# A four-stage convolution kernel: layer 1 with TensorE in a fixed order, the squares of x2 on ScalarE, weight and x2 loads issued apart

## The chip, the cores and the metric

The kernel runs on one core of a Trainium2 chip. The metric is the device time of one execution in microseconds (us). The parts of a time are read from the profiled execution of the same kernel, so they add up to its span and not exactly to the median.

## The reference

The input is 16 images of 256 channels, 28 x 28 pixels. Four layers follow each other. Layer 0 is a binary 3x3 convolution with a batch norm over all images. Layer 2 is two binary 3x3 convolutions with batch norms, layer 3 is attention over the pixels. Layer 1, for each image:

```python
residual = prelu(x, a_alpha1)
z = hardsign(x + a_move)
y = prelu(bn(conv3x3(z, clip(a_w)), a_bn1), a_alpha2)
mix = s * x + y * (1 - s)
y = se_gate(mix) * y                # mean over pixels -> 256 to 32 -> relu -> 256 -> sigmoid
y = bn(y * residual, a_bn2) + residual          # called x2 until the last line below
z2 = hardsign(y + f_move)
u = prelu(bn(conv1x1(z2, clip(f_w)), f_bn1), f_alpha2)
mix2 = s2 * y + (1 - s2) * u
return bn(se_gate(mix2) * u, f_bn2) + y         # x2, the input of layer 2
```

Layer 2 begins with a batch norm of x2 over all 16 images, so it needs the sums of x2 and of its squares.

## The kernel before

Layer 1's 3x3 convolution is done in a form with four transformed rows `vs` (u = 0 to 3). An image has two halves `mo` of the output channels, a half has two pairs, (1,2) and (0,3), and a pair is 24 matmuls of 0.19 us: 96 matmuls, 18.4 us per image. A pair fills one PSUM buffer, each half of the 1x1 (8 matmuls) one more, and there are three such buffers. VectorE and ScalarE turn pairs into rows, PReLU, sums for the gate, the gates themselves, x2, and the next image's input. The loop is software-pipelined: image b's 3x3, image b-1's gate, x2 and 1x1, image b-2's second gate. `hid` and `gate` are the names of the gate's two small matmul groups.

```python
for b in range(B + 2):
    # now: b < B;  one: 0 <= b-1 < B;  two: 0 <= b-2 < B;  ahead: b+1 < B
    conv_pair(b, 0, ...)        # pair (1,2) of half 0
    unit_a(b - 2)               # 1x1's result: u, and its relu rn, on ScalarE
    enter(b + 1)
    unit_b(b - 2)               # PReLU of u, with its sum for the gate
    sum_pair(b, 0); conv_pair(b, 0, 0, 0)
    h = gates_hidden(b)         # sums -> hid (TensorE) -> relu (ScalarE)
    conv_pair(b, 0, 1, 3)
    transform(b + 1)            # next image's vs
    g = gates(h)                # gate (TensorE) -> four sigmoids -> scaling
    branch1_a(b - 1, g); rows_out(b, 0); branch1_b(b - 1); load_x(b + 2)
    ...                         # half 1: pair (1,2), prelu_out(b, 0), residual, sum_pair
    conv_pair(b, 1, ...)        # pair (0,3) of half 1
    branch2(b - 2, g)           # x2 complete, bn_stats of it on VectorE, stored
    conv1x1(b - 1)
    rows_out(b, 1); prelu_out(b, 1)
    ...                         # one step of layer 2's weights in images 2 to 6
```

(The conditions `if now` and so on are cut.) A scheduler decides at build time in which order each engine gets its instructions; the statements only give it a priority. So TensorE's order need not be the order of the text.

## Time and profile before

| part, from the profiled execution | us |
|---|---|
| layer 1's loop: first 3x3 matmul (164.66) to the end of the last (528.17) | 363.5 |
| drain: from there to layer 2's first matmul (563.52) | 35.3 |
| entry: layer 2's first binary convolution, up to the start of the second (724.61) | 161.1 |
| everything else (layer 0 ahead, second binary convolution and attention behind) | 618 |
| median of the runs | 1179.3 |

The first three rows are what the change touches. Two more lines than the prediction shows are needed. The first is the page's summary of the chain that ended last, its share of the span by engine:

```profile
PE 64%; DVE 14%; ACT 3%; DMA 2%; issue 1%; SPq 0%; DVEq 0%; ACTq 0%
```

The second is the windows view over one late image (from, to, length, then busy us and instructions of TensorE, weight loads, VectorE, ScalarE, GpSimd, then clock, DMA share and GB/s):

```profile
401.71:425.10 23.39, 22.40 (x121) 21.71 (x120) 21.80 (x42) 14.78 (x22) 0.53 (x1) 1.00 0.25 87
```

VectorE is busy 21.8 of 23.4 us: it hardly has air, which fits the 14% of the chain that are its own.

### The profile page before, as it was taken

How to read it: one execution, taken by the hardware profiler on the slowest of the kernel's cores; microseconds unless marked ns; L12 is line 12 of the kernel's file. 1: busy time of each engine (PE TensorE's matmuls, PEld its weight loads, DVE VectorE, ACT ScalarE, POOL GpSimd, SP SyncE). 2: the span in 40 equal slices, each digit the busy share in tenths (PEclk: the TensorE clock that was granted, in tenths of full speed). 3: DMA queues.
4: the chain of work that ended last, by engine and by line, in shares of the span. 5: the costliest groups of instructions: out<-in, count | busy, mean ns of one | idle time of the engine just before them, and what ended most of it. 6: DMA issues, size and time to landing. Idle time of an engine off the chain costs nothing.

```text
span 1178.2 us, 15695 instructions
## 1 busy us (share of the span) xinstructions
PE 1113.0 (94%) x6015; PEld 944.0 (80%) x6019; DVE 817.7 (69%) x1438; ACT 692.3 (59%) x1041; POOL 142.7 (12%) x139
## 2 busy tenths in 40 slices
PE   6999999999999999994889999999999999999995
PEld 6999989999899989993789998999965545545542
DVE  3854378999999999875366665666683676576665
ACT  5644536667766665654455553555567767767752
POOL 2000000000100000000000000000004434434421
PEclk9999999999999999996989999999999999999998
DMA  7643331223221321011930000000013453553522
GB/s 283 217 163 125 136 111 55 69 83 127 92 83 69 107 87 68 28 48 37 410 115 32 1 1 1 1 1 1 1 41 97 110 164 110 137 163 119 131 82 84
DMA packets 25968, 111.62 MB, mean 95 GB/s; under 512 B 3552, under 2 KB 6304, under 8 KB 25888
## 3 DMA queue, kind: packets, MB, share of 16 engines
q1 hardware_dynamic: 20432, 80.85, 19.6%
q0 software_dynamic: 5456, 29.71, 8.7%
q8 instruction: 49, 0.80, 0.3%
q14 instruction: 31, 0.25, 0.1%
HBM read 65.59 MB, written 44.96 MB: 94 GB/s over the span
## 4 chain that ended last, share of the span: by engine, by line
PE 64%; DVE 14%; ACT 3%; DMA 2%; issue 1%; SPq 0%; DVEq 0%; ACTq 0%
PE cv L239 20%; PE cv L543 16%; PE sc L946 7%; PE av L967 6%; PE mi L931 4%; PE sm L1007 4%; DVE x L672 2%; DVE x L627 2%; DVE l_parts L674 2%; DVE xs L535 2%; PE cv L258 2%; PE mi L1017 2%; DVE y L576 1%; DMA st<-in_w2b_dram 1%; DMA p<-x2d 1%
## 5 line engine op out<-in xcount | busy, mean ns | idle before, releaser
L543 PE MATMUL cv<-vs,w 128*128 128x392 f32 x1536 | 302.3, 355 | 11.4 <-DVE y L576 10.6
L239 PE MATMUL cv<-fpads,wpk 128*128 128x392 f32 x1440 | 295.3, 358 | 12.5 <-DVE wpk L190 10.0
L543 PEld LDWEIGHTS cv<-vs,w 128*128 128x128 f32 x1536 | 286.1, 190 | 17.4 <-DVE y L576 14.9
L239 PEld LDWEIGHTS cv<-fpads,wpk 128*128 128x128 f32 x1440 | 273.2, 193 | 17.3 <-issue 10.4
L788 DVE SCALAR_TENSOR_TENSOR p<-r,r,cv 128x392 f32<-128x392 f32 x128 | 78.6, 614 | 80.4 <-ACT r L785 80.4
L950 ACT ACTIVATE es<-sc 112x784 f32<-112x784 f32 x112 | 87.4, 822 | 74.1 <-PE sc L946 73.9
L239 PE MATMUL cv<-fpads,wpl 128*128 128x392 f32 x576 | 124.8, 352 | 0.0
L239 PEld LDWEIGHTS cv<-fpads,wpl 128*128 128x128 f32 x576 | 108.8, 190 | 0.6
L250 ACT ACTIVATE t<-cv,rounding 128x392 f32<-128x392 f32 x96 | 56.2, 586 | 86.5 <-PE cv L239 81.7
L251 DVE TENSOR_SCALAR up<-t 128x392 fp32r<-128x392 f32 x96 | 35.0, 364 | 84.4 <-ACT t L250 84.4
L946 PE MATMUL sc<-q,k 64*112 64x392 f32 x448 | 90.5, 518 | 2.2 <-DVE k L938 1.6
L785 ACT ACTIVATE r<-cv 128x784 f32<-128x784 f32 (+1 forms) x66 | 52.9, 805 | 60.0 <-PE cv L258 58.1
L967 PE MATMUL av<-es,va 112*64 112x392 f32 x448 | 80.8, 499 | 0.0
L946 PEld LDWEIGHTS sc<-q,k 64*112 64x112 f32 x448 | 36.3, 174 | 43.5 <-issue 18.3
L960 POOL TENSOR_TENSOR sum<-sum,es 112x784 f32<-112x784 f32 x32 | 68.4, 2138 | 2.5
L967 PEld LDWEIGHTS av<-es,va 112*64 112x64 f32 x448 | 29.6, 136 | 47.4 <-issue 44.6
L103 DVE TENSOR_TENSOR vs<-pad 128x840 fp32r<-128x840 bf16 (+1 forms) x68 | 64.0, 975 | 0.9 <-ACT pad L514 0.9
L938 DVE COPY k<-mi 64x784 f32<-64x784 f32 x16 | 15.6, 976 | 66.3 <-ACT q L937 66.3
L449 ACT CAST n<-cv 128x784 int16<-128x784 f32 x32 | 26.0, 813 | 54.7 <-DVE l_parts L448 24.1
L640 PE MATMUL cv<-z,fw 128*128 128x392 f32 x256 | 51.4, 350 | 5.0 <-ACT z L631 5.0
L657 ACT ACTIVATE u<-cv,c_bn,s_bn 128x784 f32<-128x784 f32 x31 | 31.2, 1006 | 41.5 <-PE cv L640 41.5
L640 PEld LDWEIGHTS cv<-z,fw 128*128 128x128 f32 x256 | 46.9, 193 | 5.6 <-ACT z L631 5.5
(229 smaller groups left out, 1650.7 us busy)
## 6 DMA issues: line engine op xcount, KB each, us to landing
xs<-in_x_dram SPq DMA_DIRECT2D x32, 784.0 KB, 4.4
x2d<-x POOLq DMA_DIRECT2D x16, 784.0 KB, 3.6
xd<-p SPq DMA_DIRECT2D x16, 784.0 KB, 3.3
out_dram<-p SPq DMA_DIRECT2D x15, 784.0 KB, 5.2
p<-x2d SPq DMA_DIRECT2D x13, 784.0 KB, 15.6
p<-x2d POOLq DMA_DIRECT2D x13, 784.0 KB, 9.2
n0d<-n POOLq DMA_DIRECT2D x16, 392.0 KB, 2.7
n<-n0d SPq DMA_DIRECT2D x16, 392.0 KB, 3.1
```

The costliest lines, as they stand in the source:

```text
L103: V.tensor_tensor(o, a, b, op)
L239: T.matmul(pss[j][:, mo, :HN].rearrange("p (a b) -> p a b", b=S), lhsT=lhsT, rhs=pads[:, j // 2 % 2, k, r:r + HR, c:c + S], start=start, s ...
L250: A.activation(r, pss[j][:, 0, :HN], AF.Identity, bias=rounding, scale=1.0 / PACK)
L543: T.matmul(ps.rearrange("p (a b) -> p a b", b=S), lhsT=w[:, k, c, u, mo * P:(mo + 1) * P], rhs=vs[:, b % 2, u, k, :, c:c + S], start=(n == 0),
L640: T.matmul(ps[:, h, :HN], lhsT=w[:, k, mo * P:(mo + 1) * P], rhs=z2[b][:, k, h * HN:(h + 1) * HN], start=(n == 0), stop=(n == 3),)
L785: A.activation(r[:, mo], ps[:, mo, :HN], AF.Relu, scale=-1.0)
L788: V.scalar_tensor_tensor(p, r[:, mo], beta[:, mo:mo + 1], ps[:, mo, :HN], ALU.mult, ALU.add)
L931: T.matmul(ps[:, h, :HN], lhsT=wqk[:, k, :], rhs=x[b][:, k, h * HN:(h + 1) * HN], start=(k == 0), stop=(k == 1),)
L946: T.matmul(ps[:MC, h, :HN], lhsT=k_[rows, c * MC:(c + 1) * MC], rhs=qs[b][rows], start=True, stop=True)
L950: A.activation(e, ps[:MC, :, :HN], AF.Exp, scale=0.125)
L960: (V if late else nc.gpsimd).tensor_tensor(sums[b, late], sums[b, late], e, ALU.add)
L967: T.matmul(ps[64 * h:64 * h + 64, :HN], lhsT=w, rhs=e[:, h, :], start=start, stop=stop)
```

## The change

It has four parts, and each has its aim. (1) bn_stats of x2 leave VectorE; the sum of x2 rides on the operation that makes it, and the squares go to ScalarE. (2) In layer 1 TensorE gets exactly the order of the statements, and these are put into a new order: the gate right after the first pair, the 1x1 in the middle of the second half, the unit in the same iteration; fillers keep TensorE's clock up in the drain. (3) Loads of weights and of x2 are issued apart from the work, a few steps ahead. (4) The gate's biases become weight rows, so that one sigmoid serves four gates. Smaller edits go along: the 1x1 takes its matmuls by halves of `z`, in the last image one scaling of `y` moves to VectorE, and the two rows `up` and `vp` share one buffer, `uv`. The core of the diff:

```diff
@@ branch2: squares
-    V.scalar_tensor_tensor(v, us.pop((b, k))[0], g[:, k:k + 1], v, ALU.mult, ALU.add)
-    for i in range(2):
-        V.bn_stats(mom1.part(2 * b + i, k), v[:, i * HN:(i + 1) * HN])
+    V.scalar_tensor_tensor(v, us.pop((b, k))[0], g[:, k:k + 1], v, ALU.mult, ALU.add,
+                           accum_out=sum_x2[:, k, b:b + 1])
...
+    A.activation(full("rn", "square", 4), x2[b][:, k, :], AF.Square, bias=shift[:, k:k + 1],
+                 accum_out=sum_sq[:, k, b:b + 1])
@@ gates
-    for i, b2 in enumerate((pv("a_se_b2"), pv("f_se_b2"))):
-        for k in range(2):
-            A.activation(g[:, i, k:k + 1], ps[:, k, i:i + 1], AF.Sigmoid, bias=b2[:, k:k + 1])
+    A.activation(g.rearrange("p i k -> p k i"), ps, AF.Sigmoid)
@@ the loop (conditions cut)
-for b in range(B + 2):
+with tc.manual_schedule(engines={ET.PE}):
+  for b in range(B + 2):
     conv_pair(b, 0, ...)                     # pair (1,2); in the drain: keep_busy(14)
-    unit_a(b - 2); enter(b + 1); unit_b(b - 2)
-    sum_pair(b, 0); conv_pair(b, 0, 0, 0)
     h = gates_hidden(b)                      # now after 24 matmuls of the image
+    sum_pair(b, 0); conv_pair(b, 0, 0, 0)
+    enter(b + 1)
+    g = gates(h)                             # now after 36
     conv_pair(b, 0, 1, 3)
...
+    conv_pair(b, 1, ...)                     # pair (1,2) of half 1
+    prelu_out(b, 0); load_x(b + 2); transform(b + 1)
+    conv1x1(b - 1)                           # now after 72
+    late()                                   # sums of layer 2's weights
+    sum_pair(b, 1); conv_pair(b, 1, ...)     # pair (0,3)
+    unit_a(b - 1); residual(b + 1); rows_out(b, 1); unit_b(b - 1); prelu_out(b, 1)
@@ entry of layer 2
-for b in order[3:]:
-    x2[b] = pt[b]
-    nc.sync.dma_start(out=x2[b], in_=x2d[b])
+def sign2a(i, rows, out):
+    sign2(x2[order[i]], sg1, bg1, rows, out)
+    if rows.stop == S and i + 5 < B:
+        load_p(i + 5)
+for i in (3, 4):
+    load_p(i)
+...            # the first two weight loads of w2b are issued right behind these
```

## The prediction

> **What bounds the kernel now.** I read the page first (whose engine is full), then the stages, then the chain that ended last, then the timeline where it leaves TensorE.
>
> ```profile
> PE 1113.0 (94%) x6015; PEld 944.0 (80%) x6019; DVE 817.7 (69%) x1438; ACT 692.3 (59%) x1041; POOL 142.7 (12%) x139
> PEclk9999999999999999996989999999999999999998
> ```
>
> ```profile
> 594.50:857.00 262.50, 262.18 (x1382) 256.12 (x1383) 162.65 (x320) 138.39 (x181) 0.00 (x0) 0.99 0.05 14
> ```
>
> TensorE looks full, but the average hides layer 1 (about 160 to 562 us). The second fence is the windows view (start and end, length, then busy us of TensorE, weight loads, VectorE, ScalarE, GpSimd; clock; DMA): in the two binary convolutions TensorE really is full, 262.2 of 262.5 us. The clock row dips just once, at 530 to 560 us. So I split the time in three: layer 1's loop, its drain, the entry of layer 2.
>
> *Loop.* The chain of waits over one late image (start, us, what):
>
> ```profile
> 345.88 9.19 PE cv L543 x47
> 355.07 0.34 PE hid L477 x4
> ...
> 357.41 0.17 DVE gates L103
> ...
> 363.53 1.89 DVE xs L535 x2
> ...
> 366.89 1.48 DVE l_parts L674 x3
> 368.38 1.07 DVE y L576 x2
> 369.45 0.04 issue
> 369.49 2.54 PE cv L543 x12
> ```
>
> The image lasts 369.49 - 345.88 = 23.6 us. The last 12 us of it are VectorE working in order from the gates to the `y` that frees a PSUM buffer; the moments of x2 (bn_stats, L674) stand in front of that `y`. TensorE alone would need 18.4 us for 96 convolution matmuls (9.19 per 48), 2.86 for the 16 of the 1x1 and 0.7 for the gates: 21.9. The first image, which has neither, ends at 164.7 + 18.4 = 183.1; the fifteen from there to 528.2 took 345 us, 23.0 each. VectorE has little air, one wait of 1.55 us per image, for the sigmoid (timeline of another late image):
>
> ```profile
> 404.21 0.16 DVE L103 TENSOR_TENSOR gates<-gates,s_bn 128x4 f32<-128x4 f32 x1 [1.55 <-ACT gates L610]
> ```
>
> *Drain.* From the last 3x3 matmul (518.85 + 9.32 = 528.2) to layer 2's first (563.5) 35.3 us pass, mostly latency, and TensorE cools down:
>
> ```profile
> 505.68 3.03 PE L640 MATMUL cv<-z,fw 128*128 128x392 f32 x16
> 515.76 0.50 PE L477 MATMUL hid<-g,se 128*128 128x2 f32 x4
> ...
> 536.07 1.01 PE L477 MATMUL hid<-g,se 128*128 128x2 f32 x4 [5.04 <-DVE g L103]
> 543.66 4.78 PE L640 MATMUL cv<-z,fw 128*128 128x392 f32 x16 [4.96 <-ACT z L631]
> ```
>
> The same work takes 4.78 instead of 3.03 and 1.01 instead of 0.50.
>
> *Entry of layer 2.* The chain names two transfers, the TensorE timeline shows the hole:
>
> ```profile
> 562.00 14.33 DMA p<-x2d
> ...
> 576.41 14.66 DMA st<-in_w2b_dram
> ```
>
> ```profile
> 584.14 0.52 PE L258 MATMUL cv<-up,unpack 128*128 128x392 f32 x2
> 593.52 1.01 PE L207 MATMUL sumabs<-ones,ab 128*128 128x1 f32 x4 [8.87 <-DVE ab L201]
> 594.40 4.68 PE L239 MATMUL cv<-fpads,wpk 128*128 128x392 f32 x15
> ```
>
> The second convolution's weights were issued behind 13 loads of x2 (10 MB) and landed at 591. The first convolution runs from 563.52 to 717.4 = 153.8 us, the second, with no weights to make, from 724.61 to 863.1 = 138.5. So 15.4 us are lost: 8.9 idle, some 2 cold, the rest sums of weights between the steps.
>
> **What the Trainium skill says.** "DMA: Bandwidth & Descriptors", section "Queues, rings and completion order": on each DMA engine descriptors are consumed in ring order. The trace agrees: a 384 KB load that elsewhere lands in 3.7 us took 14.7 behind the x2 loads. "TensorE: Matmul & The Clock Gate", Part 1 (the HAM clock gate): idle for about 3.4 us the array falls to half clock; the trace's 0.50 to 1.01 agrees. The same page, "Architectural detail": ScalarE and VectorE are strict FIFO, which is why a bn_stats in front of `y` counts. "ScalarE: Activation LUTs", "What ACT_TABLE_LOAD costs": 280 ns + 0.833 N with a pointer bias, so 933 ns at N = 784 (the trace has 938 for such a Relu), and 1283 ns for a table load (trace 1.28 us).
>
> **The change, part by part.**
>
> 1. *Squares on ScalarE.* Four bn_stats per image leave VectorE, 4 x 0.47 = 1.9 us from start to start. Two Squares with an accumulator come to ScalarE. What an accumulator costs there, the attention shows:
>
> ```profile
> 954.50 0.50 ACT L1001 ACTIVATE junk<-sm 128x392 f32<-128x392 f32 x1
> 954.87 0.21 ACT L1001 ACTIVATION_READ_ACCUMULATOR junk<-sm 128x1 f32 x1
> 955.12 0.53 ACT L1001 ACTIVATE junk<-r 128x392 f32<-128x392 f32 x1
> ```
>
> The read follows 0.37 after the start and takes 0.25 to the next start. A Square of 784 should step like the Relus of that size, 0.84 to 0.89, and 0.25: two are 2.2 us per image. On VectorE the sum of x2 rides free: its operations with an accumulator step 0.95 as those without.
>
> 2. *Fixed order.* The gate's first matmuls move from behind 48 matmuls to behind 24, the 1x1 into the middle. The order of instructions shows what VectorE does then: rows out 1.07, two transforms 1.9, PReLU 0.95, sums 0.15, that is 4.07 us, before the gate's input is ready. I follow it from H, the start of the gate's first matmul, with the start-to-start steps of the trace. First matmul and 12 convolution matmuls 2.6, then second matmul, sigmoid (one for four) and scaling 1.1: VectorE goes on at H + 3.7. It then has 14.6 us (x2 1.9, x 1.92, rows 1.07, two transforms, PReLU and both halves of the next-but-one input 4.8, sums 1.1, two of unit 1.9, residual 1.9). Meanwhile ScalarE, which gets the rows at H + 8.7, has rn 0.8, squares 2.2, t 0.6, u and rn 1.8 in this order: unit's input is there at H + 14.1, where VectorE has been ready since 13.5; 0.6 wait. So the next image's rows start at 3.7 + 14.6 + 0.6 = H + 18.9 and the next gate at + 4.1 = 23.0. TensorE's own way: the sums of the pair end at H + 13.5 and free PSUM (0.8 after the 1x1 is done), plus 48 matmuls 9.2 = 22.7. I expect 23.0 us per image: the loop moves from PSUM to the gate, and little is gained against 23.4 to 24. In the five images that make layer 2's weights (sign and Abs ahead of rn on ScalarE, 1.6 us; packing 0.55 on VectorE) I get 24.1, where before the first of them ran at 22.7. Sum: first image 18.4, second 22.5, 5 x 24.1, 7 x 23.0, last two 22 each = 366 against 363.5 now (164.7 to 528.2), so about 3 us lost, 5 either way.
>
> 3. *Drain.* Counted from the last 3x3 matmul: rows and rn 2.1, PReLU and gate input 3.6, gates at 5.8 (one sigmoid for four, 0.26 for 0.72; warm), y 6.9, x 8.3, z 9.5, 1x1 from 9.6 to 12.6 (the first half of z suffices, warm), unit 15.8, gates 18.4, x2 20.4, squares 21.8. The table load for the root now stands behind the squares: 23.0; root and constants 1.5: 24.5; sign and first matmul 0.9: 25.4. Against 35.3 that is 10 us gained.
>
> 4. *Entry of layer 2.* Weights now stand behind five x2 loads and 0.4 MB, 4.4 MB. At the about 420 GB/s of this stretch they land 12 us after the issue, some 10 us after TensorE starts, and are wanted in the fifth step (about 16 us). No wait; of the 15.4 us stay the sums of weights, 7 x 0.45 = 3. Gain 12.
>
> 5. *Layer 0, bias rows, attention.* The early weight loads meet a TensorE that is already full (266 of 270 us busy between 30 and 300); 0. Bias rows are in point 3.
>
> Sum: 1179.9 + 3 - 10 - 12 = 1161.
>
> **Rivals.** (a) *TensorE becomes the bound in layer 1*: 21.9 per image if the wait in the loop is less than I add up. For it: VectorE's sum falls to 19.9, ScalarE's is 17; both under 21.9. Against it: VectorE stands idle between gate and sigmoid, as it does now (1.55 us per image), and more in the new order. It would end layer 1 some 14 us earlier: 1144 to 1148. (b) *ScalarE's squares are worse than 2.2 us, or collide with the weight steps*: 24 us per image, 10 us more, 1171. For it: rn and u stand behind them in order. (c) *The weight loads still come late*, because the queue waits for a buffer of x2 ahead of them: only 2 or 3 of the 12 us, 1170. Against it: those buffers are read in the first three images, before the weights are wanted. (d) *Cooling goes on*: the fillers end 1.5 us before the 1x1; a gap too short for it.
>
> **Range and chances.** The gains of drain and entry (22 us, give or take 3) I hold for safe; the loop is the open term, 5 us either way, and (a) is likelier than (b), since a fixed order was presumably chosen by looking. The 2% line is 1156.3, 5 us under my sum: 28% faster. Slower by 2% would need 1203: 1%. Eight in ten: 1150 to 1169.
>
> **What would show it.** In the loop: pitch of the images 23.0, and 24 in images 2 to 6; TensorE's waits named after the gate input `g` instead of `y`. A pitch near 22 says (a). In the drain: 25 us from the last 3x3 to layer 2, 1x1 at 3.0 us, no dip of the clock, the table load behind the squares. At the entry: no hole of 8.9 us, first convolution about 142 us. It would be wrong if layer 1's end moved by more than 8 us, or if a new wait for x2 loads came up in the first ten steps of layer 2.

## More of the kernel before

Every time quoted is a median of executions.

The loop ends with the last 3x3 matmul. Where the 1x1 stands behind an image's last pair, as in this kernel, the 1x1 of image 14 (about 3 us) therefore falls into the drain; where it stands in the middle of an image, it is counted in the loop.

## The result, and the profile after

The changed kernel took 1185.57 us (median of 4 runs, 1183.89 to 1187.65) against 1179.3 for the kernel before. The ratio is 1.0054, 95% interval 1.0035 to 1.0074: the same within 2%, but on the slow side, where 1161 had been predicted. Ratios here are the mean time of one kernel's fast runs over that of the other's fast runs of the same rounds, so not quite the ratio of the medians.

| part | before | predicted | after | change |
|---|---|---|---|---|
| loop | 363.5 | 366 | 390.6 | +27.1 |
| drain | 35.3 | 25.4 | 26.0 | -9.3 |
| entry | 161.1 | 149 | 151.5 | -9.6 |

The three changes sum to +8.2; the spans of the two profiled executions differ by 7.7. The changed kernel's profiled execution is the slowest of its four (1187.65 us), so a difference of 2 us between the parts of two kernels can lie in the execution. Drain and entry did about what they were meant to do. The loop is where the time went.

*Drain after*, TensorE's timeline (start, us, what, idle before it):

```profile
555.87 2.97 PE L346 MATMUL unused<-idle 128*128 128x512 bf16 x13
559.42 0.61 PE L507 MATMUL hid<-g,se 128*128 128x2 f32 x4 [0.58 <-DVE g L103]
...
565.62 3.23 PE L670 MATMUL cv<-z,fw 128*128 128x392 f32 x16
...
581.84 5.96 PE L252 MATMUL cv<-fpads,wpk 128*128 128x392 f32 x30
```

The fillers (`unused`) stand where TensorE had been idle, and the 1x1 takes 3.23 us where it took 4.78.

*Entry*, the windows view from the start of the first binary convolution to that of the second, first of the kernel before, then of the changed one:

```profile
563.52:724.61 161.09, 151.91 (x793) 145.62 (x794) 97.59 (x198) 80.10 (x107) 0.00 (x0) 0.97 0.25 94
```

```profile
581.84:733.30 151.46, 149.83 (x794) 143.65 (x794) 97.69 (x198) 80.71 (x108) 0.00 (x0) 1.00 0.26 101
```

TensorE's idle time in it falls from 9.2 to 1.6 us (length less busy time), and its own work is 2.1 us shorter because the clock stays at 1.00.

*Loop after.* The page's chain still gives VectorE a large share, and TensorE's timeline now shows it waiting in two places, ahead of the gate (16.7 us over the loop) and ahead of the last pair (6.8 us for `rn`):

```profile
PE 62%; DVE 16%; ACT 4%; issue 2%; DMA 2%; DVEq 0%; ACTq 0%
```

```profile
215.85 0.61 PE L507 MATMUL hid<-g,se 128*128 128x2 f32 x4 [1.50 <-DVE g L103]
216.32 3.49 PE L573 MATMUL cv<-vs,w 128*128 128x392 f32 x12
...
294.35 0.61 PE L507 MATMUL hid<-g,se 128*128 128x2 f32 x4 [1.82 <-DVE g L103]
...
418.28 0.61 PE L507 MATMUL hid<-g,se 128*128 128x2 f32 x4 [0.16 <-DVE g L103]
418.75 2.52 PE L573 MATMUL cv<-vs,w 128*128 128x392 f32 x12
...
432.20 9.37 PE L573 MATMUL cv<-vs,w 128*128 128x392 f32 x48 [0.79 <-ACT rn L533]
...
442.13 0.61 PE L507 MATMUL hid<-g,se 128*128 128x2 f32 x4 [0.56 <-DVE g L103]
```

From one `hid` to the next is one image: 442.13 - 418.28 = 23.85 us. In images 1 to 7, in most of which layer 2's weights are made too, it is 25.1 to 26.9. After six of the eight waits of 1.3 us or more the next 12 matmuls run slow, 3.49 instead of 2.52 in the lines above; the trace shows half the clock (0.50) granted for 3.4 us there.

The same image on VectorE (and the two squares on ScalarE):

```profile
421.85 0.16 DVE L103 TENSOR_TENSOR gates<-gates,s_bn 128x4 f32<-128x4 f32 x1 [1.82 <-ACT gates L638]
...
425.99 0.33 SPq L356 DMA_DIRECT2D xs<-in_x_dram  x1
...
427.83 0.94 ACT L707 ACTIVATE square<-x,shift 128x784 f32<-128x784 f32 x1
...
428.77 0.94 ACT L707 ACTIVATE square<-x,shift 128x784 f32<-128x784 f32 x1
...
429.70 0.66 ACT L594 ACTIVATE t<-cv,c_bn,s_bn 128x392 f32<-128x392 f32 x1
430.26 0.99 ACT L686 ACTIVATE u<-cv,c_bn,s_bn 128x784 f32<-128x784 f32 x1
430.90 1.03 DVE L541 SCALAR_TENSOR_TENSOR xs<-n,l_r,xs 128x784 f32<-128x784 int16 x1 [0.94 <-DMA xs<-in_x_dram]
431.15 0.99 ACT L533 ACTIVATE rn<-cv,nc,ns 128x784 f32<-128x784 f32 x1
```

Here VectorE waits 1.82 us for the gates, which the instruction next in its order needs, then 0.94 us for a load. Over the loop the waits for the gates come to 43.0 us, where it was 16.3 before, and those for the load to 7.3. The last pair's PSUM buffer is the 1x1's first half, which `rn` frees at 431.15 + 0.99 = 432.14; the pair starts at 432.20. The two squares stand ahead of `t`, `u` and `rn` on ScalarE. The windows view of the same image:

```profile
418.28:442.13 23.85, 22.49 (x120) 21.74 (x121) 20.34 (x38) 16.73 (x24) 0.53 (x1) 1.00 0.25 85
```

VectorE's work did fall, from 21.80 to 20.34 us per image. But the image did not get shorter. VectorE now stands idle 23.85 - 20.34 = 3.5 us in it, where it had been 1.6.

This gave four theories. T1: the fixed order puts the gate and the 1x1 in places where TensorE waits for VectorE's chain. T2: the squares on ScalarE hold up `t`, `u` and `rn`. T3: the sums for the weights come too late in the fixed order, and VectorE waits for them in line. T5: TensorE's slow clock after its waits is itself a large part. (T4, the wait for the load of `xs`, has no run of its own; it comes below.)

### The profile page after: what moved, and what is told of

Same layout as the page of the kernel before. It is cut to its first block, busy times and chain, and to the rows that moved or that the text cites. A ratio compares the mean times of both kernels' runs of the same rounds, so it can differ in the third digit from the quotient of the medians.

```text
span 1185.9 us, 15794 instructions
## 1 busy us (share of the span) xinstructions
PE 1129.0 (95%) x6069; PEld 954.7 (81%) x6075; DVE 794.7 (67%) x1410; ACT 714.2 (60%) x1053; POOL 146.0 (12%) x144
## 4 chain that ended last, share of the span: by engine, by line
PE 62%; DVE 16%; ACT 4%; issue 2%; DMA 2%; DVEq 0%; ACTq 0%
PE cv L252 20%; PE cv L573 12%; PE sc L1014 7%; PE av L1035 6%; PE mi L999 4%; PE sm L1075 4%; DVE vs L103 2%; PE unused L346 2%; PE cv L271 2%; PE mi L1085 2%; PE cv L670 2%; DMA xs<-in_x_dram 2%; DVE y L606 2%; DVE uv L596 2%; DVE xs L565 1%
## 5 line engine op out<-in xcount | busy, mean ns | idle before, releaser
L573 PE MATMUL cv<-vs,w 128*128 128x392 f32 x1536 | 309.9, 361 | 8.3 <-ACT rn L533 6.8
L573 PEld LDWEIGHTS cv<-vs,w 128*128 128x128 f32 x1536 | 293.0, 194 | 13.5 <-ACT rn L533 9.5
L264 DVE TENSOR_SCALAR uv<-t 128x392 fp32r<-128x392 f32 x96 | 35.0, 364 | 82.8 <-ACT t L263 82.8
L1075 PEld LDWEIGHTS sm<-wv,p 128*112 128x112 f32 x448 | 46.7, 178 | 5.0 <-issue 2.6
L1089 DVE TENSOR_TENSOR p<-mi,p 128x784 f32<-128x784 f32 x30 | 29.2, 974 | 31.5 <-PE mi L1085 31.1
L271 PE MATMUL cv<-uv,unpack 128*128 128x392 f32 x192 | 49.9, 341 | 0.0
```

The lines of the kernel that those rows point to most:

```text
L271: T.matmul(pss[j][:, mo, :HN], lhsT=unpack[mo], rhs=bs[j], start=False, stop=True, skip_group_check=(mo == 0))
L573: T.matmul(ps.rearrange("p (a b) -> p a b", b=S), lhsT=w[:, k, c, u, mo * P:(mo + 1) * P], rhs=vs[:, b % 2, u, k, :, c:c + S], start=(n == 0),
L1075: T.matmul(ps[:MC, c * 64:(c + 1) * 64], lhsT=x[b][:, k, c * MC:(c + 1) * MC], rhs=wv[:, k, :], start=(k == 0), stop=(k == 1),)
```

## The experiments

All sixteen kernels of the experiments gave correct results. Parts in us as in the tables above; the median of the runs last.

| run | loop | drain | entry | time |
|---|---|---|---|---|
| before | 363.5 | 35.3 | 161.1 | 1179.3 |
| changed | 390.6 | 26.0 | 151.5 | 1185.6 |
| entry only | 363.5 | 35.7 | 151.5 | 1168.6 |
| squares only | 350.0 | 38.1 | 160.0 | 1166.1 |
| changed, without squares | 393.0 | 26.0 | 151.7 | 1188.0 |
| changed, old loop | 348.3 | 32.1 | 151.5 | 1150.1 |
| gate 12 matmuls later | 386.3 | 27.4 | 151.5 | 1183.5 |
| weight sums first | 386.5 | 25.8 | 151.5 | 1182.6 |
| old statements, fixed order | 351.6 | 32.2 | 151.4 | 1154.9 |
| new statements, free order | 371.1 | 26.9 | 151.5 | 1168.9 |
| gate 24 later, 1x1 last | 350.7 | 31.3 | 151.5 | 1152.2 |
| squares late | 379.6 | 27.4 | 151.5 | 1176.7 |
| old loop, new last image | 351.6 | 27.4 | 151.5 | 1148.5 |
| the same, no fillers | 351.7 | 28.8 | 151.5 | 1150.9 |
| 1x1 last, gate early | 411.8 | 31.6 | 151.5 | 1216.1 |
| gate 12 later, squares late | 377.6 | 27.1 | 151.6 | 1175.6 |
| fillers ahead of the gate | 387.1 | 27.4 | 151.5 | 1186.0 |
| gate 24 later, 1x1 in the middle | 448.4 | 30.6 | 151.6 | 1243.4 |

### Which part of the change costs, and which pays

**Entry only.** The kernel before, with the loads issued apart in all layers and the entry's new order; loop, squares and gates untouched, but for the shared buffer `uv`.

```diff
 # the kernel before, plus:
+class Step: ...            # load() and work() apart
+steps = load_ahead(steps, 2)
+def sign2a(i, rows, out): ...   # the next x2 load behind each image's sign
```

> The kernel before with only the entry's part (loads apart from the work, x2 in steps, no drain or loop part). If the entry is worth the 9.4 us that the two traces show, the time is 1168 to 1172 us, the first binary convolution takes 143 to 146 us, and layer 1's loop stays at 363 to 365 us and the drain at 35. If the gain needs the new loop (x2 written earlier), the first binary convolution stays over 148 us and the time over 1174 us.

1168.56 us (ratio 0.9906, interval 0.989 to 0.9923), loop and drain as before, entry 151.5. The first binary convolution by itself, from its first matmul to its last, takes 144.9 us, where it took 154.5: as written. The entry's 9.6 us are there on their own, and they need nothing of the new loop.

**Squares only.**

```diff
 # the kernel before, plus:
-    V.bn_stats(mom1.part(2 * b + i, k), v[:, i * HN:(i + 1) * HN])
+    A.activation(..., x2[b][:, k, :], AF.Square, ..., accum_out=sum_sq[:, k, b:b + 1])
```

> The kernel before with only the squares moved from bn_stats on VectorE to ScalarE. Theory 1 (the fixed order is the cause of the longer loop): the loop gets 0 to 6 us shorter than 363.5, the time is 1173 to 1180 us. Theory 2 (squares on ScalarE are the cause, they hold up t, u and rn): the loop gets 5 us or more longer, 1184 us or more.

1166.13 us (ratio 0.9891, interval 0.9874 to 0.9907). The loop fell by 13.5 us, more than either theory had. T2 as a general statement has fallen: on ScalarE the squares do no harm in the old loop.

**Changed, without squares**: bn_stats back on VectorE, the new loop kept.

```diff
 # the changed kernel, with:
-    A.activation(..., x2[b][:, k, :], AF.Square, ..., accum_out=sum_sq[:, k, b:b + 1])
+    V.bn_stats(mom1.part(2 * b + i, k), v[:, i * HN:(i + 1) * HN])
```

> The changed kernel with bn_stats back on VectorE, the fixed order kept. Theory 1: the loop closes through VectorE and the gate, so with 1.9 us more on VectorE per image it gets longer still, 392 to 420 us, and the time is 1188 to 1215 us. Theory 2: the loop shrinks to 380 us or less, the time to 1175 us or less.

1187.96 us, loop 393.0. The time is just under what T1 had written, far from T2's. But VectorE's 1.9 us more per image, some 28 over the loop, show as 2.4 only: taking the squares off ScalarE also takes away what their place costs there (11 us, see *squares late*) and VectorE's waits for `xs`. **Changed, old loop** undoes the other factor: the old order of statements, TensorE free, everything else of the change kept.

```diff
 # the changed kernel, with:
-with tc.manual_schedule(engines={ET.PE}):
-    ...   # the new order
+for b in range(B + 2):
+    ...   # the order of the kernel before
```

> The changed kernel with the loop's old order of statements and TensorE's order left to the scheduler; squares on ScalarE, bias rows and the entry stay. Theory 1: the loop is 358 to 366 us again, the drain 32 to 36 us, the entry 9 us shorter than before: 1164 to 1171 us. Theory 2: the loop stays over 375 us and the time over 1178 us.

1150.14 us (ratio 0.9751, interval 0.9734 to 0.9767): 2.5% faster than the kernel before, and the loop even shorter than T1 expected. With the run *entry only* this makes a square of four loops:

| loop, us | bn_stats on VectorE | squares on ScalarE | gain of the squares |
|---|---|---|---|
| old loop | 363.5 | 348.3 | 15.2 |
| new loop | 393.0 | 390.6 | 2.4 |

So the new loop costs 42.3 us with the squares on ScalarE and 29.5 without, less the 6 and 10 us that it gives in the drain (about 3 us of each are only the 1x1 that is counted in the loop now): 36 and 20 us in all. The upper row is not the squares alone, because its two kernels also differ in the sigmoids and the small edits; the squares by themselves gave 13.5 us. And the new loop swallows the squares' gain. Why the old loop gets all of it shows the windows view of one image of that run, and its chain:

```profile
414.39:436.32 21.93, 21.93 (x121) 21.84 (x121) 20.18 (x39) 16.23 (x24) 0.53 (x1) 1.00 0.27 92
```

```profile
PE 74%; DVE 4%; ACT 3%; issue 2%; DMA 2%; POOL 1%; ACTq 0%; POOLq 0%; DVEq 0%
```

TensorE is busy 21.93 of 21.93 us. VectorE does the same 20.2 us of work as in the changed kernel, but TensorE bounds the loop, and VectorE's share of the chain is 4% instead of 16%.

### Is it fixing the order, or the order that was fixed?

**Gate 12 matmuls later.** The gate's groups after 36 and 48 matmuls of the image instead of 24 and 36.

```diff
+    sum_pair(b, 0); conv_pair(b, 0, 0, 0)
     h = gates_hidden(b)
-    sum_pair(b, 0); conv_pair(b, 0, 0, 0)
     enter(b + 1)
+    conv_pair(b, 0, 1, 3)
     g = gates(h)
-    conv_pair(b, 0, 1, 3)
```

> The changed kernel with the gate's two matmul groups 12 matmuls (about 2.4 us) later in the fixed order: the first after 36 matmuls of the image instead of 24, the second after 48 instead of 36. Theory 1 (TensorE stands still for the gate's sums, 17.3 us in 15 waits, and runs slow after it): those waits fall under 5 us, the 12 matmuls after them take 2.4 to 2.6 us again, the loop falls from 390.6 to 365 to 378 us and the time to 1160 to 1174 us. Rival (the chain only waits elsewhere: the later gate makes z later, and the 1x1 waits instead): loop and time stay within 5 us of the changed kernel's.

1183.46 us, loop 386.3: loop and time are the rival's, though the wait moved to another place than the one it named. In TensorE's timeline the wait ahead of the gate has gone in the late images, and the one ahead of the last pair has grown, from 0.79 us for `rn` to 1.36 for `uv`:

```profile
423.51 3.04 PE L670 MATMUL cv<-z,fw 128*128 128x392 f32 x16
427.91 11.60 PE L573 MATMUL cv<-vs,w 128*128 128x392 f32 x60 [1.36 <-DVE uv L596]
439.47 0.61 PE L507 MATMUL hid<-g,se 128*128 128x2 f32 x4
```

That pair now waits 1.36 us in every late image for the PSUM buffer that VectorE's `uv` frees. The Trainium skill, "Perfetto Trace Analysis", section "Optimization Strategy", says that the same gap repeating on the engine that should be saturated can mean too little PSUM for the next tile; the trace agrees. T1 for the gate alone has fallen.

**Weight sums first.** The sums of layer 2's weights ahead of the gate, instead of behind the 1x1.

```diff
+    late()
     h = gates_hidden(b)
...
     conv1x1(b - 1)
-    late()
```

> The changed kernel with only the weight steps' sums (PE's sumabs and what follows on VectorE) put ahead of the gate in the fixed order instead of behind the 1x1. Theory 3 (VectorE waits in order for sums that TensorE does late, which makes the weight images 25 to 27 us long): the weight images fall to 24 to 25 us each, the loop by 5 to 12 us, the time to 1174 to 1181 us. If the weight images are long only because of the work on ScalarE and VectorE, the time stays at 1183 to 1188 us.

1182.56 us, loop 4.1 us shorter: between the two ranges. But the five stretches from gate to gate that T3 wanted to shorten, images 2 to 6, take 25.9 us on average, as against 26.0 in the changed kernel; the gain lies ahead of them and behind. T3, as the reason why these images are long, has fallen.

**Old statements, fixed order.** The old loop, but with TensorE's order fixed near the one that the scheduler had chosen for it: `hid` after 48 matmuls, `gate` 12 later, the 1x1 behind the last pair.

```diff
 # the changed kernel with the old loop, plus:
+with tc.manual_schedule(engines={ET.PE}):
     ...
-    h = gates_hidden(b)
     conv_pair(b, 0, 1, 3)
+    h = gates_hidden(b)
+    conv_pair(b, 1, 0, 1)
     g = gates(h)
```

> The loop of old statements (as in the run with the old order), but with TensorE's order fixed as the scheduler had about put it: the gate's first group after 48 matmuls of the image, its second 12 later, the 1x1 behind the image's last pair. If the place of the gate and of the 1x1 is what costs, and not fixing as such: loop 346 to 354 us, time 1148 to 1157 us. If any fixed order costs (the scheduler's freedom is worth it): loop over 365 us and time over 1165 us.

1154.85 us, loop 351.6, as expected. A fixed order as such costs 3 us of loop, not 42.

**New statements, free order**: only the one line that fixes TensorE taken out of the changed kernel.

```diff
-with tc.manual_schedule(engines={ET.PE}):
+if True:
     for b in range(B + 2):
```

> The changed kernel with its own new order of statements, but TensorE's order left to the scheduler. If the fixed place of the gate is the cause, the scheduler puts it later and the loop falls to 350 to 370 us, the time to 1145 to 1167 us (fillers of the drain may land elsewhere). If the new order of statements itself (VectorE's and ScalarE's order, loads later) is the cause, the loop stays over 380 us and the time over 1175 us.

1168.88 us, loop 371.1, in between and just outside both ranges. The scheduler put the gate 39 matmuls into the image, but left the 1x1 in the middle, and TensorE waits 0.9 us for `uv` ahead of the last pair of a late image.

### Two places that hang together

**Gate 24 later, 1x1 last.** The changed kernel's fixed order with both places changed. (The unit and the sums of the weights stand behind the 1x1, so they move along.)

```diff
     sum_pair(b, 0)
+    conv_pair(b, 0, 0, 0); conv_pair(b, 0, 1, 3)
     h = gates_hidden(b)
-    conv_pair(b, 0, 0, 0)
     enter(b + 1)
+    conv_pair(b, 1, 0, 1)
     g = gates(h)
-    conv_pair(b, 0, 1, 3)
...
-    conv1x1(b - 1)
     sum_pair(b, 1); conv_pair(b, 1, ...)     # pair (0,3)
+    conv1x1(b - 1)
```

> The changed kernel's statements with a fixed order on TensorE in which the gate comes after 48 and 60 matmuls of the image and the 1x1 behind the image's last pair (as in the fixed order that took 351.6 us), so that both places change together. If the two places on TensorE are the whole of it, the loop is 348 to 356 us and the time 1145 to 1157 us. If the order of the statements on VectorE and ScalarE costs too, as the free schedule with the new statements (371 us) suggests, the loop is 360 to 375 us and the time 1157 to 1172 us.

1152.15 us, loop 350.7, TensorE without a wait in a late image:

```profile
426.45 3.03 PE L670 MATMUL cv<-z,fw 128*128 128x392 f32 x16
429.32 9.28 PE L573 MATMUL cv<-vs,w 128*128 128x392 f32 x48
438.43 0.50 PE L507 MATMUL hid<-g,se 128*128 128x2 f32 x4
```

This gives back 39.9 of the 42.3 us, or, with the drain, 34.6 of 36.2. Is one of the two places enough?

**1x1 last, gate early**: only the 1x1 moves, behind the last pair.

```diff
-    conv1x1(b - 1)
     late()
     sum_pair(b, 1); conv_pair(b, 1, ...)     # pair (0,3)
+    conv1x1(b - 1)
```

> The changed kernel with only the 1x1 moved in the fixed order, from the middle of the second half to behind the image's last pair; the gate stays after 24 and 36 matmuls. If the 1x1's place is the cause by itself (it takes two of the PSUM buffers just ahead of the last pair): loop 350 to 362 us, time 1145 to 1158 us. If the early gate needs the early 1x1 (the unit's sums, about 6 us after the 1x1, go into the next image's gate, which comes 4.6 us into that image): the waits ahead of the gate grow to 2 us or more in every image, and the loop stays over 380 us.

1216.07 us, loop 411.8, worse than the changed kernel. The next gate needs the sum of the 1x1's unit, and now only one pair, 24 matmuls, lies between the two, so TensorE waits 2.14 us for it:

```profile
313.07 3.03 PE L670 MATMUL cv<-z,fw 128*128 128x392 f32 x16
316.66 4.81 PE L573 MATMUL cv<-vs,w 128*128 128x392 f32 x24 [0.56 <-ACT rn L533]
323.61 0.61 PE L507 MATMUL hid<-g,se 128*128 128x2 f32 x4 [2.14 <-DVE g L103]
```

**Gate 24 later, 1x1 in the middle**: the good fixed order above, with only the 1x1 put back (so its unit stays where it is there).

```diff
+    conv1x1(b - 1)
     sum_pair(b, 1); conv_pair(b, 1, ...)     # pair (0,3)
-    conv1x1(b - 1)
```

> The fixed order that gave 350.7 us of loop (gate after 48 and 60 matmuls, 1x1 last), with only the 1x1 put back to the middle, ahead of the last pair. If the gate's place alone is worth the 40 us, the loop is 348 to 358 us and the time 1144 to 1158 us. If the two places hang together (the 1x1 then comes 12 matmuls, 2.4 us, after the gate's second group, while x2 and its signs need about 6 us from there), TensorE waits 2 to 4 us for z in each image: loop 385 to 415 us, time 1180 to 1212 us.

1243.37 us, loop 448.4. The direction was as written, the size was not: besides the wait for `z`, TensorE waits for `y` at the next image's start, and it ran at a mean clock of 0.91 over 200 us of this loop.

```profile
433.01 5.59 PE L670 MATMUL cv<-z,fw 128*128 128x392 f32 x16 [2.84 <-ACT z L662]
...
444.69 9.37 PE L573 MATMUL cv<-vs,w 128*128 128x392 f32 x48 [1.25 <-DVE y L606]
```

| loop, us | 1x1 in the middle | 1x1 last |
|---|---|---|
| gate after 24 and 36 matmuls | 390.6 | 411.8 |
| gate after 48 and 60 matmuls | 448.4 | 350.7 |

Either move alone makes it worse by 21 or 58 us, both together better by 40. (The left column counts one 1x1 more in the loop, about 3 us, and in the lower row the unit and the weight sums stand later too. Half the gate's move alone, 12 matmuls, had brought 4 us.) Two dependences tie them: the gate needs the unit of the 1x1 before it, and the 1x1 needs `z`, which needs the gate. Each wants its distance; the early pair of places gives both too little, the late pair gives both enough.

### The rest of the loop's cost

**Squares late**: the squares behind the unit in the order of statements.

```diff
-    branch2(b - 2, g[:, 1])     # with the squares
+    branch2(b - 2, g[:, 1])     # without
...
     unit_a(b - 1); residual(b + 1); rows_out(b, 1)
+    squares(b - 2)
     unit_b(b - 1)
```

> The changed kernel with the two squares (1.9 us on ScalarE) moved behind the 1x1's unit in the order of statements, nothing else. Theory 2 (in the fixed order the squares stand ahead of t, u and rn on ScalarE, and the last pair waits there for its PSUM buffer): the 0.2 to 0.8 us waits for rn ahead of the last pair vanish, 6.8 us in all, and the gate's waits shrink; loop 375 to 385 us, time 1170 to 1181 us. Otherwise (another engine's order is behind it) loop and time stay within 3 us of the changed kernel's 390.6 and 1185.6.

1176.73 us, loop 379.6. T2 holds inside the new loop: the last pair no longer waits (in the changed kernel 6.8 us in all), and the gate's wait grows to 0.94 in a late image. VectorE's waits for `xs`, 7.3 us in the changed kernel, have gone as well, so the 11 us are not the PSUM buffer's alone:

```profile
423.40 9.27 PE L573 MATMUL cv<-vs,w 128*128 128x392 f32 x48
433.61 0.61 PE L507 MATMUL hid<-g,se 128*128 128x2 f32 x4 [0.94 <-DVE g L103]
```

**Gate 12 later and squares late** together, the two diffs above in one kernel.

> The changed kernel with the gate 12 matmuls later and the squares behind the unit, the 1x1 left in the middle. Alone the first gave 386.3 us and the second 379.6 us of loop. If each takes away the wait that the other leaves (0.95 us for the gate, 1.4 us for the last pair's buffer), the gains are more than added: loop 352 to 368 us, time 1148 to 1166 us. If they only add up: loop 373 to 378 us, time 1168 to 1175 us.

1175.62 us, loop 377.6: the two gains do not even add up (13.0 us of 4.3 and 11.0), and the time is 0.6 us above what was written. Again a wait of 1.1 us ahead of the gate.

**Fillers ahead of the gate**: idle work for TensorE where it would wait and cool.

```diff
+    if 1 <= b <= 7:
+        keep_busy(6)
     h = gates_hidden(b)
```

> The changed kernel with six fillers (about 1.3 us of idle work for TensorE) just ahead of the gate's first matmuls in images 1 to 7, where it waits 1.3 to 2.3 us. If part of the longer loop is the slow clock after those waits (12 matmuls took 3.2 to 3.8 us instead of 2.4 in several images), they take 2.4 to 2.6 us again, the loop falls by 3 to 8 us and the time to 1178 to 1183 us. If the waits themselves are all, the loop stays within 2 us of 390.6, or grows by a few.

In the trace the 12 matmuls behind each of these gates take 2.52 or 2.53 us, where in the changed kernel the first three took 3.76, 3.49 and 3.18:

```profile
212.43 1.47 PE L346 MATMUL unused<-idle 128*128 128x512 bf16 x6
214.08 0.61 PE L507 MATMUL hid<-g,se 128*128 128x2 f32 x4 [0.19 <-DVE g L103]
214.55 2.52 PE L573 MATMUL cv<-vs,w 128*128 128x392 f32 x12
```

The clock was repaired and the loop of the profiled execution was 3.5 us shorter, but the timed runs were not faster: 1186.03 us (1184.06 to 1190.47), where 1178 to 1183 had been written. In this execution images 2 to 6 took 25.4 us on average instead of 26.0, but in two later images VectorE waited longer for the load of `xs` than in the changed kernel (0.94 and 0.64 there), so that part of the gain was lost again:

```profile
426.00 1.03 DVE L541 SCALAR_TENSOR_TENSOR xs<-n,l_r,xs 128x784 f32<-128x784 int16 x1 [2.22 <-DMA xs<-in_x_dram]
452.17 1.03 DVE L541 SCALAR_TENSOR_TENSOR xs<-n,l_r,xs 128x784 f32<-128x784 int16 x1 [1.83 <-DMA xs<-in_x_dram]
```

That T5 is a large part is not shown.

### A version that beats both

**Old loop, new last image**: the old statements with TensorE free, in the last image the 1x1 ahead of its last pair, and the last two iterations in the changed kernel's fixed order with fillers.

```diff
+    if b == B - 1:
+        conv1x1(b - 1); branch2(b - 2, g[:, 1])
     sum_pair(b, 1); conv_pair(b, 1, ...)     # pair (0,3)
+    if b == B - 1:
+        unit_a(b - 1)
...
+with tc.manual_schedule(engines={ET.PE}):
+    for b in range(B, B + 2):
+        ...   # the changed kernel's order
```

> The old order of statements with TensorE free (loop 348.3 us, drain 32.1 us), but for the last image the 1x1 ahead of its last pair and the unit behind it, and the two iterations after it in the changed kernel's order with fillers. If the drain's gain of 6 us comes from the place of the 1x1 and the unit, the drain falls to 26 to 28 us and the time to 1143 to 1147 us; if it is paid back in the last image, the time stays at 1149 to 1152 us.

1148.53 us (ratio 0.974, interval 0.9718 to 0.9762). The time lies between the two ranges. The drain fell by 4.6 us, into the range written, but the loop grew by 3.3, about the last 1x1, which is counted in it now; together they are 379.1 us instead of 380.4. The version is not told apart from the run with the old loop (interval 0.9734 to 0.9767); both beat the kernel before by 2.5%. **Without the fillers** of the last two iterations:

```diff
-    else:
-        keep_busy(14)
```

> The same without the fillers of the last two iterations. If they only keep the clock up, the first 3x3 or 1x1 matmuls after the waits run slower and the time is the same or up to 2 us longer; if TensorE works them off while real work is ready, the time is 1 to 4 us shorter.

1150.85 us, 2.3 us longer, the drain 28.8 instead of 27.4. The fillers pay a little; without them loop and drain together are 380.4 us, as in the old loop, so the new last image gains nothing by itself.

## Why the prediction was wrong

It said 1161 us, 1150 to 1169, and the kernel took 1185.6. One of its readings is wrong, without harm to the sum: its clock row dips not once but also at 589 to 618 us (an 8), at the entry's hole. By its own steps:

**Drain (step 3)**: right. 25.4 us predicted, 26.0 measured, with the 1x1 warm. It had written that the clock would not dip; half of it (0.50) was granted from 562.1 to 565.5 us, over the fillers just ahead of the 1x1.

**Entry (step 4)**: right in its mechanism, 2.4 us too hopeful. Of the 12 us, 9.6 came. It had left 3 us for the sums of the weights. In the trace the eight steps from the first sum to the last take 638.00 - 597.92 = 40.1 us, where a step without sums takes 4.34, so 34.7: they cost 5.4. The step forgot that TensorE waits for VectorE's `ab` at three of the sums, 1.4 us in all.

**Layer 0 and attention (step 5)**: right, no part of the difference.

**Squares (step 1)**: the cost per image was near, 2.2 us predicted on ScalarE and 1.87 measured (427.83 to the start of `t` at 429.70). What they are worth was left to the sum of step 2, and there it was lost; in the old loop it is 13.5 us.

**Fixed order (step 2)** is the step that failed: "I expect 23.0 us per image", 24.1 in the five weight images, "366 against 363.5". The mechanism it named is what the trace shows: TensorE's waits carry the name `g` and no longer `y`, and the loop closes through the gate. The sizes are wrong. Counted from gate to gate, its loop was 23.0 to the first gate, then 22.5, five of 24.1, seven of 23.0, one of 22.0, and 17.4 behind the last. Measured: 24.7; 26.0; five with a mean of 26.0; then eight with a mean of 24.0 (against 22.9); 18.1. So 13.1 of the 24 us too few are in the first six gate-to-gate distances, 8.7 in the next eight, 2.4 at both ends.

What stands in place of the sum, term by term. In the late image shown above VectorE went on behind the gates at 422.05, H + 3.8; predicted was 3.7. The wait of VectorE between there and the end was predicted as 0.6 us, for the unit; measured were 0.94 us, for the load of `xs`, which starts at 425.99, right behind VectorE's last `x` operation, and lets VectorE go on at 430.90. From the rows to the next gate it predicted 4.07; measured 418.28 - 413.84 = 4.44. In the weight images it took 1.1 us more than normal; measured are 2.1 more than the eight images behind them. The trace shows where they lie. In one of these images the way from the rows to the gate is 320.88 - 315.26 = 5.6 us (5.8 on average of the five), 1.2 more than the 4.44 above:

```profile
315.26 1.16 DVE L606 SCALAR_TENSOR_TENSOR y<-cv,s_bn,uv 128x392 f32<-128x392 f32 x2
316.33 0.98 DVE L206 SCALAR_TENSOR_TENSOR wpk<-sg 128x384 fp32r<-128x384 bf16 x1
317.23 1.02 DVE L103 TENSOR_TENSOR vs<-pad 128x840 fp32r<-128x840 bf16 x1
...
320.14 0.62 DVE L596 SCALAR_TENSOR_TENSOR uv<-cv,s_bn,t 128x392 f32<-128x392 f32 x1
320.68 0.15 DVE L103 TENSOR_TENSOR g<-g,g 128x4 f32<-128x4 f32 x1
```

The packing of the weights (`wpk`) takes 0.90 there, where 0.55 was predicted, and one `uv` of the new pair (0.54), which the predicted 4.07 does not hold, stands ahead of the gate's last addition. Besides, in three of the five (images 2, 3 and 5) the slow clock makes VectorE go on at H + 4.7 to 5.0 instead of 3.8, 0.7 us on average. Together that is about the 2.1 us. It is read off the trace; no run changes VectorE's order alone. TensorE's own way was too short as well: the last pair's buffer was to be freed by the sums at H + 13.5, and it is freed by `rn`, behind the squares, at 432.14, H + 13.9.

The larger mistake lies ahead of the arithmetic. The step compared the new loop with the old loop as it was, 363.5 us, and found 3 us lost. It did not ask what the old loop would do with the squares alone. The numbers for it were in the prediction: VectorE's work falls to 19.9 us and TensorE needs 21.9. Rival (a), TensorE as the bound at 21.9 us per image, was thus right for the old loop (21.93 measured) and wrong for the new one, to which it was applied. Measured against that, the new loop loses 42 us, 36 with the drain, and the guess that it "was presumably chosen by looking" is what kept the range too low.

Rival (b), squares in the way of the weight steps, holds for part of it: inside the new loop their place costs 11 us, not because a square is slow but because they stand ahead of `t`, `u` and `rn`, on which a PSUM buffer waits (and, as said, VectorE's waits for `xs` go with them). Rival (c) is refuted by the entry-only run. Of (d): in the last version the fillers were worth 2.3 us of time, 1.3 of them in the drain, and "a gap too short for it" does not fit the loop, where gaps of 1.3 to 2.3 us were followed by half the clock.

Why the order binds so hard, the Trainium skill says in "TensorE: Matmul & The Clock Gate", section "Step-by-step: what each phase is for": only weight loads are pulled ahead, the matmuls stay in program order. The trace agrees: ahead of `hid` TensorE stood 1.3 to 2.3 us in images 1 to 7, though the 12 matmuls behind it wait for nothing that the gate gives. With 44 matmuls of the image ahead of it, as the free scheduler has it in the old loop, VectorE's chain has its time.

Left open: T4, the waits for `xs`, 7.3 us in eleven images. They stand in VectorE's way from gate to gate, and no run gives `xs` more than its four buffers or loads it earlier. Open is also why the new statements in a free order still lose 23 us of loop against the old ones.

## What to carry to other kernels

A part of a change that frees the busiest engine must be valued against the loop as it would be with that part alone; here the squares alone were worth 13.5 us of loop, and another part of the same change lost them and 27 more. If an order is fixed by hand, write down for each small matmul in a dependent chain how much work stands between its inputs and it, and move such places together: each of two moves alone made the loop longer by 21 or 58 us, both together shorter by 40. And run a fixed order against the free scheduler before keeping it.

## What the Trainium skill lacked or had wrong

- "TensorE: Matmul & The Clock Gate", Part 1, gives about 3.4 us idle as what halves the clock. Here waits of 1.3 to 2.3 us, once per image, were followed by 12 matmuls in 3.2 to 3.8 us instead of 2.5 in four of the first five images, with half the clock (0.50) granted for 3.4 us; fillers in the waits brought 2.52. Two waits of 2.0 us were not, so the length of the wait alone does not decide it here. (Its part on micro-idling between groups of matmuls points this way, without a length.)
- "ScalarE: Activation LUTs" gives the cost of an activation, and the Square of 784 with its 0.93 to 0.94 us agrees. It has no cost for an accumulator output: each is a separate read of 0.18 to 0.19 us, which sets in ahead of the activation's end, so that two squares with their reads take 1.87 us.
- No page says that an order fixed on TensorE has to be checked against the two-way tie of a gate and the matmuls that it feeds; the four loops of 350.7, 390.6, 411.8 and 448.4 us show how much lies in it.
